# A third buffer for evicted value tiles, inverse roots by Newton's steps on VectorE, and gate and up weights requested ahead of half the tokens

## The chip, the core and the metric

The kernel runs on one core of a Trainium2 chip. TensorE (PE) multiplies matrices into PSUM, VectorE (DVE) and ScalarE (ACT) work on SBUF and PSUM, GpSimd (POOL) works on SBUF, and SyncE (SP) issues most of the transfers. Each engine runs its own instructions in order, and semaphores make it wait for another engine or for a transfer. The metric is the device time of one execution in microseconds; lower is better.

## The reference

Two layers run over 4 sequences of 512 tokens of width 128. Each layer normalizes, runs an attention and a mixture of experts on the same normalized tokens, and adds their gated product:

```
x = L0_attn_x                                   # (4, 512, 128)
xn = _layernorm(x)                              # (x - m) / sqrt(v + 1e-5)
s = _L0_attn_ref(xn, ...)                       # 16 heads, segments of 64, a memory carried on
g = _silu(_L0_ffn_ref(xn, ...))                 # 8 experts, top 2, and a shared one
x = x + s * g
xn = _layernorm(x)
s = _L1_attn_ref(xn, ...)                       # 16 heads, 16 channels of cosine weights
g = _silu(_L1_ffn_ref(xn, ...))                 # 8 experts with gelu, top 2
return x + s * g
```

In the first attention, q, k and v of a sequence are each reshaped to (segments, heads, 64, 64) without a transpose. A segment's output is a sigmoid gate's mix of a softmax attention inside the segment and of a read of a memory M, Z, which elu(k)+1 and v of every segment update.

## The kernel before

**Stages.** Tokens are held as 16 tiles of 128 (`self.x`, tile n belongs to sequence n // 4). First come the layer's first experts (`norm_ffn0`, up to about 76 us of the profile), then the first attention (`attn0`, up to about 300 us) with the second layer's normalization and routing of half the tokens woven in, then the second experts (`ffn1`), then the second attention.

**Loads.** `load_first` (L119) issues, on SP's queue, 12 of the 16 token tiles (the tiles 1, 3, 5, 7 go on ACT's), then `wg` (L136) and `wu` (L138), the gate and up weights of 8 experts, 256 KB each, then `wd` and the attention's weights. `norm_ffn0` needs `wg` at its first expert pair (`glu`, L441) and the tiles 8 to 11 in `sums(2)` after that pair.

**The first attention.** 32 segments n, eight to a sequence, are taken in a loop written out by hand (L834); the order on each engine is the order of the code. A segment's block does: `values(n + 2)` (requests the v of a later segment from DRAM), `scores(n + 1)` (PE `sc`, then DVE `E`, the capped scores), `memory(n)` (PE `mm`, DVE `rm` and `t`, POOL times the gate), `elu` (DVE), `turned` (PE transposes `tn`, which ACT evicts as four `attT` copies and `sk`), `update(n)` (PE `mu`, DVE `mz`), a slot `between.get(n - 0.5)`, `attend(n)` (PE `dot`; DVE `rd`, `t`, `sums`; POOL twice), four chunks of the next projection, a slot `between.get(n - 0.25)`, at n % 4 == 2 `output` (PE `po`, DVE `sg`, POOL adds to `x`), and a slot `between.get(n)`.

**The chunks** are projections for a later group of four segments. At n % 4 == 3 they are four value chunks (`chunk_v`, L616): a matmul `pv` into PSUM, an eviction to an SBUF tile `vt` (by ACT from the third half-sequence on, by DVE before), and a transfer of `vt` to the DRAM tensor `vd`, from where `values` fetches it in another layout. The pool `a0` has two buffers to a tag, so the eviction of the third chunk waits for the first chunk's transfer, and the fourth for the second's. At the other n the chunks are `pp`, of q or k, which ACT evicts to `pj`.

**PSUM.** All of these results share four buffers (`wide`, L347). A matmul group waits until the last reader of its buffer's former content is through, so a late eviction holds up a later matmul that has nothing else to do with it.

**The second norm.** `norm_sums` (L304) takes mean and variance of four tiles in eight DVE instructions. `roots(0, 2)` takes sqrt(v + eps) of eight tiles on ACT, which has to load another function table for it and load the old one again; `scale(0, 2, False)` takes the reciprocal on DVE, and `normed` applies it. The dictionary handed to `attn0` (L2413) says where:

```
18: [(first.sums, 0)], 19: [(first.sums, 1)],
20: [(first.roots, 0, 2)], 20.5: [(first.scale, 0, 2, False), (first.normed, 0)],
21: [(first.turned, 0), (first.normed, 1)],
```

Of the kernel before, what the change touches and what calls it, by code (L numbers as in the profile page):

```python
# [12 lines left out]
F32 = mybir.dt.float32  # L13
I32 = mybir.dt.int32
# [3 lines left out]
ALU = mybir.AluOpType  # L18
# [3 lines left out]
P = 128  # L22
B, S, D = 4, 512, 128
# [3 lines left out]
NT = 16  # L27
EPS = 1e-5
# [80 lines left out]
class Kernel:  # L109
# [8 lines left out]

    def load_first(self, pool, pool_attn, crossed=False):  # L119
        nc, i = self.nc, self.i  # L120
        for n in range(NT):
            eng = nc.scalar if n in (1, 3, 5, 7) else nc.sync
            eng.dma_start(out=self.x[:, n, :], in_=self.tiles_of(i["L0_attn_x"], n))

        self.wr = pool.tile([P, NE], F32, name="wr")
        nc.gpsimd.dma_start(out=self.wr, in_=i["L0_ffn_Wr"])
        self.ebias = pool.tile([P, NE], F32, name="ebias")
        nc.gpsimd.dma_start(out=self.ebias, in_=i["L0_ffn_expert_bias"].partition_broadcast(P))
        self.sg = pool.tile([P, 128], F32, name="sg")
        nc.gpsimd.dma_start(out=self.sg, in_=i["L0_ffn_Sg"])  # L130
        self.su = pool.tile([P, 128], F32, name="su")
        nc.gpsimd.dma_start(out=self.su, in_=i["L0_ffn_Su"])
        self.sd = pool.tile([P, D], F32, name="sd")
        nc.gpsimd.dma_start(out=self.sd, in_=i["L0_ffn_Sd"])
        self.wg = pool.tile([P, NE, F0], F32, name="wg")
        nc.sync.dma_start(out=self.wg, in_=i["L0_ffn_Wg"].rearrange("e d f -> d e f"))  # L136
        self.wu = pool.tile([P, NE, F0], F32, name="wu")
        nc.sync.dma_start(out=self.wu, in_=i["L0_ffn_Wu"].rearrange("e d f -> d e f"))  # L138
        self.wd = pool.tile([P, NE // 2, D], F32, name="wd")
        nc.sync.dma_start(  # L140
            out=self.wd, in_=i["L0_ffn_Wd"].rearrange("(j e) f d -> (e f) j d", e=2)
        )

        self.wqkv = []
        for w in ("Wq", "Wk", "Wv"):
            t = pool_attn.tile([P, H0 * DK], F32, name=f"l0{w}")
            nc.sync.dma_start(out=t, in_=i[f"L0_attn_{w}"])
            self.wqkv.append(t)
        self.wo = pool_attn.tile([P, H0, D], F32, name="l0wo")
        for p in range(2):  # L150
            nc.sync.dma_start(
                out=self.wo[p * 64 : p * 64 + 64],
                in_=i["L0_attn_Wo"].rearrange("(c v) d -> v c d", v=DK),
            )
        be = i["L0_attn_betas"][0, :, 0].rearrange("(hp a p) v -> a p hp v", a=2, p=2)
        self.gate = pool_attn.tile([P, 4, 2, DK], F32, name="gate")
        for p in range(2):
            for a in range(2):


                for x in range(2):
                    rows, cols = (a, slice(x, 4, 2))
                    if crossed:
                        rows, cols = (a + x) % 2, slice(2 * a, 2 * a + 2)
                    nc.sync.dma_start(
                        out=self.gate[rows * 64 : rows * 64 + 64, cols, p, :],
                        in_=be[a, p, x:4:2].partition_broadcast(64),
                    )
# [141 lines left out]

    def norm_root(self, mv, rstd, tiles):
        self.act1(rstd[:, tiles], mv[:, tiles, 1], AF.Sqrt, bias=self.eps)

    def norm_scale(self, mv, rstd, tiles, root=True):
        if root:
            self.norm_root(mv, rstd, tiles)
        self.vec1(self.nc.vector.reciprocal(rstd[:, tiles], rstd[:, tiles]))
# [261 lines left out]
    def attn0(self, xnT, g0, stack, between):  # L579
# [4 lines left out]
        nc, tc = self.nc, self.tc  # L584
# [4 lines left out]
        pool = stack.enter_context(tc.tile_pool(name="a0", bufs=2))  # L589
# [9 lines left out]
        for k in range(4):  # L599
            t = pool.tile([P, 4, 2, DK + 1], F32, name=f"vone{k}", bufs=1)  # L600
# [5 lines left out]
        def project(h):  # L606


            if h >= 2 * B:
                return []  # L610
            qkv[h] = dst = [
                pool.tile([P, 32, 64], F32, name=f"pj{h}_{wi}", tag=f"pj{wi}")
                for wi in range(2)
            ]
            vd[h] = drams.tile([2, P * 16, DK], F32, name=f"vd{h}", tag="vd")
            def chunk_v(p, k):  # L616
                ps = self.narrow(f"pv{h}_{p}_{k}")
                self.mm1(
                    ps, lhsT=xnT[h // 2][:, h % 2 * 2 + p, :],
                    rhs=self.wqkv[2][:, k * S : (k + 1) * S], start=True, stop=True,  # L620
                )
                t = pool.tile([P, S], F32, name=f"vt{h}_{p}_{k}", tag="vt")
                if h > 1:
                    self.act1(t, ps, AF.Copy)
                else:
                    self.vec1(nc.vector.tensor_copy(t, ps))
                nc.sync.dma_start(
                    out=vd[h][p].rearrange("(q k c) d -> k q (c d)", k=2, c=8)[k], in_=t
                )

            def chunk(wi, cq):
                ps = self.narrow(f"pp{h}_{wi}_{cq}").rearrange("p (c k) -> p c k", c=4)
                for c4 in range(4):
                    c = cq * 4 + c4
                    for p in range(2):
                        self.mm1(
                            ps[halves[p], c4, :],
                            lhsT=self.wqkv[wi][:, c * 64 : c * 64 + 64],
                            rhs=xnT[h // 2][:, h % 2 * 2 + p, :], start=True, stop=True,
                        )  # L640
                view = dst[wi].rearrange("d k (t c) -> d (k t) c", c=16)
                self.act1(
                    view[:, :, cq * 4 : cq * 4 + 4], ps.rearrange("d c k -> d k c"), AF.Copy
                )
            qk = [(lambda wi=wi, cq=cq: chunk(wi, cq)) for wi in (1, 0) for cq in range(4)]
            v = [(lambda p=p, k=k: chunk_v(p, k)) for p in range(2) for k in range(2)]
            return v + qk if h else qk[:4] + v + qk[4:]

# [232 lines left out]
    def begin_ffn1(self, pool, psum, layer, rooms=False):  # L881


        nc, v = self.nc, self.nc.vector
        mv = pool.tile([P, NT, 2], F32, name=f"mv{layer}")
        rstd = pool.tile([P, NT], F32, name=f"rstd{layer}")
# [3 lines left out]
        xnT, acc, xn, hid, out = {}, {}, {}, {}, {}  # L890
        parts, picked, place, ids, rows, sent, got, marks = ({} for _ in range(8))
        if rooms:
# [4 lines left out]
                out=ones, in_=ones, pattern=[[1, P]], compare_op=ALU.is_ge, fill=0.0,  # L897
# [37 lines left out]
        def roots(first, end):  # L935
            self.norm_root(mv, rstd, slice(first * 4, end * 4))

        def scale(first, end, root=True):
            self.norm_scale(mv, rstd, slice(first * 4, end * 4), root)

# [188 lines left out]
        def joined(b, part):  # L1129
# [5 lines left out]
                self.vec1(v.tensor_add(acc[b], *got[b]))  # L1135

        return SimpleNamespace(**{f.__name__: f for f in (
            sums, roots, scale, normed, turned, hidden, logits, chosen, up, down,
            split, placed, marked, send, up2, down2, fetch, joined,
        )}, xnT=xnT, acc=acc)  # L1140

# [1239 lines left out]
    def run(self):  # L2381
        nc, tc, ctx = self.nc, self.tc, self.ctx
# [14 lines left out]
        with tc.tile_pool(name="wf1", bufs=1) as wf1, tc.tile_pool(name="f1", bufs=1) as f1:  # L2397
# [11 lines left out]
            first = self.begin_ffn1(f1, None, 1, True)  # L2409
            self.four = True  # L2410
            with tc.tile_pool(name="ap0", bufs=1, space=PSUM) as self.banks:
                left = self.attn0(xnT, g0, stack, {
                    18: [(first.sums, 0)], 19: [(first.sums, 1)],  # L2413
                    20: [(first.roots, 0, 2)], 20.5: [(first.scale, 0, 2, False), (first.normed, 0)],
                    21: [(first.turned, 0), (first.normed, 1)],
                    21.5: [(first.turned, 1), (first.split, 1)],
                    21.75: [(first.hidden, 0), (first.hidden, 1)],
                    23: [(first.logits, 0), (first.logits, 1), (first.chosen, 1)],
                    24: [(first.placed, 1)], 25: [(first.chosen, 0)],
                    30.5: [(first.up, 0, 0)],  # L2420
                })
            self.four = False
            with tc.tile_pool(name="ap", bufs=1, space=PSUM) as psum:
# [33 lines left out]
                f = first  # L2457
# [95 lines left out]
```

## Time and profile before

| | us |
|---|---|
| runs | 707.73, 707.6, 710.62 (median 707.73) |
| profiled execution | 707.65 |
| span of its instructions | 705.7 |
| PE, DVE, ACT, POOL busy | 662.5, 498.5, 488.9, 344.7 |
| mean granted TensorE clock | 0.991 |

The profile shows one execution. Instructions carry the line of the kernel that made them, but the recording helpers make most PE and ACT instructions appear under the helpers' lines L336 and L339, so they are told apart by their tiles. Row times count from the span's start. "Idle before" is the time in which the engine stood still before an instruction, with the event that ended it.

### The profile page before, as it was taken

Reading aid. Unit: us, or ns where it says so; the run is one execution under the profiler, and the core shown is the slowest. Engines: PE = TensorE matmul, PEld = TensorE weight load, DVE = VectorE, ACT = ScalarE, POOL = GpSimd, SP = SyncE. Lnnn points to the kernel's source line nnn. Section 1 sums busy time; section 2 is a strip of 40 time slices with the busy share of each in tenths; the row PEclk is TensorE's granted clock in tenths of the full one; section 3 lists DMA queues with packets and bytes.
Section 4 is the critical chain, followed back from the end, with each engine's and each line's share of the span. In section 5 each row is a group of like instructions: output and inputs, shape, how many; then the busy total and the mean of one; then the engine's idle time right before and its main releaser. Section 6 shows DMA issues by size and latency. Waiting matters only on the chain.

```text
span 705.7 us, 23780 instructions
## 1 busy us (share of the span) xinstructions
PE 662.5 (94%) x10120; PEld 412.4 (58%) x10123; DVE 498.5 (71%) x1072; ACT 488.9 (69%) x809; POOL 344.7 (49%) x383
## 2 busy tenths in 40 slices
PE   7999899999999799789999999999999999999995
PEld 3666667977977768767787783332335243422324
DVE  6866375676677567874459223989897999678884
ACT  4533477786876877742553468989997899899850
POOL 7670046667677384783753333411383835230170
PEclk9999999999999998999999999999999999999999
DMA  7740252232232222100034249967949494947300
GB/s 166 161 136 0 69 144 86 55 108 78 63 95 75 63 61 64 33 3 1 1 109 147 75 150 218 260 167 171 242 153 210 115 249 143 217 136 179 76 17 20
DMA packets 85489, 79.72 MB, mean 113 GB/s; under 512 B 42640, under 2 KB 74160, under 8 KB 82304
## 3 DMA queue, kind: packets, MB, share of 16 engines
q1 hardware_dynamic: 82544, 75.39, 40.4%
q0 software_dynamic: 2256, 2.47, 1.8%
q8 instruction: 82, 1.34, 0.8%
q10 hardware_dynamic: 576, 0.26, 0.1%
q14 instruction: 31, 0.25, 0.1%
HBM read 51.62 MB, written 26.21 MB: 110 GB/s over the span
## 4 chain that ended last, share of the span: by engine, by line
PE 65%; ACT 14%; DVE 12%; DMA 3%; issue 2%; SPq 1%; POOL 0%; DVEq 0%; ACTq 0%; POOLq 0%
PE acc L336 10%; ACT e L339 8%; PE eo L336 7%; PE pp L336 7%; PE po L336 5%; PE ph L336 4%; PE b L336 3%; PE s L336 3%; PE pl L336 3%; DMA vd<-vt 2%; PE pg L336 2%; PE pu L336 2%; PE den L336 2%; PE sc L336 1%; DVE elu L689 1%
## 5 line engine op out<-in xcount | busy, mean ns | idle before, releaser
L339 ACT ACTIVATE e<-s 128x1024 f32<-128x1024 f32 x124 | 121.9, 1055 | 14.0 <-PE s L336 12.9
L336 PE MATMUL acc<-e,strip 128*32 128x512 f32 x1000 | 124.5, 598 | 0.9 <-DVE e L1946 0.9
L339 ACT ACTIVATE e<-e 128x1024 f32<-128x1024 f32 x104 | 107.3, 1094 | 0.0
L743 POOL TENSOR_TENSOR t<-t,gate 128x512 f32<-128x512 f32 x32 | 50.2, 1567 | 54.9 <-DVE t L724 54.9
L336 PEld LDWEIGHTS acc<-e,strip 128*32 128x32 f32 x1000 | 28.4, 109 | 70.0 <-issue 58.3
L781 POOL TENSOR_TENSOR t<-t,gate 128x512 f32<-128x512 f32 x32 | 49.6, 1551 | 34.2 <-DVE sums L780 27.7
L689 DVE SCALAR_TENSOR_TENSOR elu<-elu,up 128x512 f32<-128x512 f32 x60 | 46.3, 771 | 11.6 <-ACT up L339 11.4
L339 ACT ACTIVATE pj<-pp 128x512 f32<-128x512 f32 x64 | 38.0, 608 | 15.4 <-PE pp L336 14.1
L339 ACT ACTIVATE h<-ph 128x1024 f32<-128x1024 f32 x20 | 20.5, 1024 | 39.0 <-PE ph L336 32.3
L336 PE MATMUL s<-q,k 64*128 64x512 bf16 x256 | 40.9, 382 | 3.6 <-ACT e L339 3.3
L782 POOL TENSOR_TENSOR t<-t,t 128x512 f32<-128x512 f32 x32 | 42.7, 1333 | 2.5
L336 PEld LDWEIGHTS <-k 64*128 64x128 bf16 x256 | 8.7, 94 | 59.7 <-issue 58.6
L666 DVE TENSOR_TENSOR E<-sc,cap 128x512 f32<-128x512 f32 x32 | 22.0, 688 | 29.5 <-PE sc L336 29.5
L336 PE MATMUL eo<-w_out,h 128*128 128x128 f32 x320 | 39.7, 278 | 0.0
L336 PEld LDWEIGHTS eo<-w_out,h 128*128 128x128 f32 x320 | 37.6, 192 | 3.4 <-issue 2.2
L339 ACT ACTIVATE elu<-pj 128x512 f32<-128x512 f32 x60 | 38.6, 643 | 0.1
L339 ACT ACTIVATE up<-pj 128x512 f32<-128x512 f32 x60 | 38.4, 640 | 0.0
L1727 POOL TENSOR_TENSOR pr<-pr,pr 128x512 f32<-128x512 f32 x14 | 22.6, 1633 | 29.7 <-DVE pr L1722 29.6
L336 PE MATMUL pp<-xnT,l0Wk 128*64 128x128 f32 x512 | 33.4, 289 | 2.4 <-ACT sk L339 1.6
L339 ACT ACTIVATE attT<-tn 128x128 f32<-128x128 f32 x100 | 19.5, 282 | 21.4 <-PE tn L702 20.5
L1634 DVE TENSOR_TENSOR second<-second,first 128x1024 f32<-128x1024 f32 x16 | 27.0, 1693 | 8.7 <-DMA second<-qf 7.3
L336 PEld LDWEIGHTS pp<-xnT,l0Wk 128*64 128x64 f32 x512 | 30.5, 146 | 4.2 <-ACT sk L339 2.6
(346 smaller groups left out, 1590.3 us busy)
## 6 DMA issues: line engine op xcount, KB each, us to landing
vd<-vt SPq DMA_DIRECT2D x32, 256.0 KB
vone<-vd SPq DMA_DIRECT2D x64, 128.0 KB
first<-qe SPq DMA_DIRECT2D x8, 1024.0 KB
second<-qf SPq DMA_DIRECT2D x16, 512.0 KB
third<-qf SPq DMA_DIRECT2D x32, 256.0 KB
qf<-qT SPq DMA_DIRECT2D x64, 64.0 KB
k<-kd SPq DMA_DIRECT2D x16, 256.0 KB
q<-qd SPq DMA_DIRECT2D x16, 256.0 KB
```

The costliest lines, as they stand in the source:

```text
L336: return self.pin(self.nc.tensor.matmul(*args, **kw))
L339: return self.pin(self.nc.scalar.activation(*args, **kw))
L666: self.vec1(nc.vector.tensor_tensor(e, ps[:, :, 0:256].rearrange("p x (hp c) -> p x hp c", hp=4), bc(bc(self.cap, 1, 4), 1, 2), ALU.min,))
L689: self.vec1(nc.vector.scalar_tensor_tensor(t, t, 1.0, up, ALU.min, ALU.add))
L743: nc.gpsimd.tensor_mul(t, t, self.gate)
L781: nc.gpsimd.tensor_mul(t, t, gate2)
L782: nc.gpsimd.tensor_add(t, t, seg[n]["t1"])
L1634: self.vec1(self.nc.vector.tensor_mul(t, t, self.first1[mm][:, two]))
L1727: self.nc.gpsimd.tensor_add(self.prod1[b, m], self.prod1[b, m], t)
```

## The change

The third edit moves the requests of the tiles 8 to 15 behind those of `wg` and `wu`. The first gives the tag `vt` three buffers in place of two. The second moves `sums(0)` from the end of segment 18 to the end of segment 14, moves `sums(1)` from the end of segment 19 to the slot before its `attend`, drops the square root and the reciprocal, and puts `newton` in the slot before `attend(20)`.

```
@@ load_first
-        for n in range(NT):
-            eng = nc.scalar if n in (1, 3, 5, 7) else nc.sync
-            eng.dma_start(out=self.x[:, n, :], in_=self.tiles_of(i["L0_attn_x"], n))
+        def tokens(first, end):
+            for n in range(first, end):
+                eng = nc.scalar if n in (1, 3, 5, 7) else nc.sync
+                eng.dma_start(out=self.x[:, n, :], in_=self.tiles_of(i["L0_attn_x"], n))
+        tokens(0, 8)
...
         nc.sync.dma_start(out=self.wu, in_=i["L0_ffn_Wu"].rearrange("e d f -> d e f"))
+        tokens(8, NT)
@@
+    def norm_newton(self, pool, mv, rstd, tiles, name):
+        v, n = self.nc.vector, tiles.stop - tiles.start
+        var, r = mv[:, tiles, 1], rstd[:, tiles]
+        half, t = (pool.tile([P, n], F32, name=f"{w}{name}") for w in ("half", "newt"))
+        self.vec1(v.tensor_scalar(half, var, EPS, -0.5, ALU.add, ALU.mult))
+        bits = pool.tile([P, n], I32, name=f"bits{name}")
+        self.vec1(v.tensor_scalar(t, var, EPS, None, ALU.add))
+        self.vec1(v.tensor_scalar(bits, t.bitcast(I32), 1, None, ALU.arith_shift_right))
+        self.vec1(v.tensor_scalar(
+            r.bitcast(I32), bits, -1.0, float(0x5F3759DF), ALU.mult, ALU.add
+        ))
+        for _ in range(3):
+            self.vec1(v.tensor_mul(t, r, r))
+            self.vec1(v.tensor_mul(t, t, half))
+            self.vec1(v.scalar_tensor_tensor(r, t, 1.5, r, ALU.add, ALU.mult))
@@ chunk_v
-                t = pool.tile([P, S], F32, name=f"vt{h}_{p}_{k}", tag="vt")
+                t = pool.tile([P, S], F32, name=f"vt{h}_{p}_{k}", tag="vt", bufs=3)
@@ begin_ffn1
+        def newton(first, end):
+            self.norm_newton(pool, mv, rstd, slice(first * 4, end * 4), f"{first}")
@@ run
-                    18: [(first.sums, 0)], 19: [(first.sums, 1)],
-                    20: [(first.roots, 0, 2)], 20.5: [(first.scale, 0, 2, False), (first.normed, 0)],
+                    14: [(first.sums, 0)], 18.5: [(first.sums, 1)], 19.5: [(first.newton, 0, 2)],
+                    20.5: [(first.normed, 0)],
```

## The prediction

> **What bounds the kernel now.** I read the page first. PE is busy 94% of the span and makes 65% of the chain that ended last, but the chain also holds ACT, DVE and transfers, so the question is where PE waits.
>
> ```profile
> PE 662.5 (94%) x10120; PEld 412.4 (58%) x10123; DVE 498.5 (71%) x1072; ACT 488.9 (69%) x809; POOL 344.7 (49%) x383
> PE 65%; ACT 14%; DVE 12%; DMA 3%; issue 2%; SPq 1%; POOL 0%; DVEq 0%; ACTq 0%; POOLq 0%
> ```
>
> The view of waits, for PE from 112 to 260 us and for ACT from 76 to 300, names what the edits aim at: ACT stands 11.5 us in front of value evictions until a transfer has read the buffer, and PE then stands for ACT (`dot <- ACT vt`, `pp <- ACT sk`).
>
> ```profile
> PE pp L336 <- ACT sk L339: 3.7, 5, 2.1
> PE dot L336 <- ACT vt L339: 3.4, 3, 1.6
> ACT vt L339 <- DMA vd<-vt: 11.5, 9, 2.5
> ```
>
> The timeline shows the worst place, segments 19 to 21 (start, length, engine): two evictions wait 1.12 and 2.49 us, `dot` starts 1.56 late, then ACT is late at every step, and two table loads around one square root make PE wait 2.06 more.
>
> ```profile
> 228.36 0.60 ACT L339 ACTIVATE vt<-pv 128x512 f32<-128x512 f32 x1 [1.12 <-DMA vd<-vt]
> 231.45 0.60 ACT L339 ACTIVATE vt<-pv 128x512 f32<-128x512 f32 x1 [2.49 <-DMA vd<-vt]
> 232.10 1.04 PE L336 MATMUL dot<-vone,E 64*64 64x65 f32 x32 [1.56 <-ACT vt L339]
> 233.07 4.97 PE L336 MATMUL pp<-xnT,l0Wk 128*64 128x128 f32 x64
> 238.71 1.28 ACT L339 ACT_TABLE_LOAD   x1
> 240.31 1.28 ACT L339 ACT_TABLE_LOAD   x1
> 243.95 1.31 PE L336 MATMUL pp<-xnT,l0Wq 128*64 128x128 f32 x20 [2.06 <-ACT sk L339]
> ```
>
> The windows view (PE, PEld, DVE, ACT, POOL busy, granted clock, transfers) says why those 64 `pp` took 4.97 us and not 3.7 as elsewhere: after the pause the clock fell to half.
>
> ```profile
> 233.00:234.00 1.00, 1.00 (x17) 0.93 (x12) 0.88 (x2) 1.00 (x6) 0.00 (x0) 0.50 0.60 223
> 267.00:268.00 1.00, 1.00 (x21) 0.88 (x23) 0.90 (x9) 0.38 (x2) 0.00 (x0) 0.50 0.55 207
> ```
>
> At the start the timeline shows PE waiting for `wg`, requested at 8.91 behind twelve token tiles.
>
> ```profile
> 8.91 0.59 SPq L136 DMA_DIRECT2D wg<-in_L_ffn_Wg_dram  x1
> 13.51 1.12 PE L336 MATMUL pg<-xnT,wg 128*128 128x512 f32 x2 [1.79 <-DMA wg<-in_L_ffn_Wg_dram]
> ```
>
> **The change part by part.** Each place is retimed by hand: rows keep their lengths and start when their last input or their engine is there.
>
> *Weights sooner: -1.15 us.* Tiles take 0.60 us each on SP, so after four of them `wg` is requested at about 3.4 instead of 8.91. It took 4.56 us to land with a full queue; even doubled it lands at 12.5, and at the same speed at 8.0, before PE is free at 11.72. PE then starts `pg` 1.75 us sooner. The second matmul group behind it, `eo`, needs `hs`, which DVE ends at 14.66, so some 0.6 is given back: `pg` of the next pair goes from 17.40 to about 16.25. From there to 63.9 PE is the whole chain, and the gain stays. What moves behind: the tiles 8 to 15, each two requests (1.2 us) later, the last before 10; `sums(2)` reads them at about 17. `wd` and all later requests on SP keep their places, and POOL's and ACT's queues are untouched. Bounds: 0 (another input is late) to -1.75.
>
> *Three tiles.* With three buffers the third eviction waits for nothing and the fourth for the first transfer, where before it waited for the second.
> - First half-sequence (DVE evicts): the third and fourth ran at 84.44 after a wait of 1.37, and PE's transposes at 86.64 waited 0.67 for the `elu` behind them. The fourth alone still starts at 84.44, so `elu` ends 0.7 sooner: -0.65.
> - Segments 3 and 11: ACT's fourth eviction goes from 121.66 to 119.32 (the first transfer lands at 119.28). PE's stalls 0.91 (`dot`) and 0.47 (`pp`) go; PE is the bound again: -1.38 each.
> - Segment 7: PE's stalls are 0.35 (`tn`) and 0.32 (`pp`), and both go: -0.7.
> - Segment 15: see the next item. Segment 23: `vt` waits there too, but PE's `lp` and DVE's routing come last: 0.
> Bounds: 0 (the waits move one tile on) to all the waits of ACT, -11.5.
>
> *`sums(0)` from 18 to 14.* Eight DVE instructions from 221.19 to 222.79 stand between `sg` and `E`. Without them PE's `pv` (224.51) starts 223.72, as `dot` follows `mu` at 223.10: -0.8. The same 1.6 us now stands after `sg` at 194.76: `E` starts 196.36 and not 194.98, `t` ends 197.93, and `pv`, whose PSUM buffer `t` frees, starts 198.08 and not 196.59: +1.5. Behind it the waits for `vt` in segment 15 (0.34 and 0.34 on PE) are gone with the three tiles, so PE is 0.95 late when segment 16's `pp` go on. Net for segment 15: +0.95.
>
> *Segments 19 to 21, with `sums(1)` and the roots moved: -5.5 with the 0.8 above.* `sums(1)` now stands before `attend(19)`: DVE 224.4 to 226.0, so its `t` ends 227.1. Queued behind it are `rd`, `t`, `elu` and `E`; PE's next `sc`, which in the changed program takes the buffer that `t` frees, is due at 227.35: hidden by the `pv`. The first transfer lands 2.06 after its request, at 227.55, so the fourth eviction ends 228.2, and `dot(20)` starts 229.7 and not 232.10. The 64 `pp` take 3.7 at full clock: `sc` at 234.0, not 237.97.
> Newton's 13 instructions follow `mz` at 231.0. The trace has no such instruction; the nearest are 128x8 ones on DVE:
>
> ```profile
> 276.50 0.17 DVE L1052 TENSOR_SCALAR many<-own 128x8 f32<-128x8 f32 x1
> 276.71 0.17 DVE L1054 TENSOR_TENSOR sums<-sums,many 128x8 f32<-128x8 f32 x1
> 276.79 0.16 DVE L1057 SCALAR_TENSOR_TENSOR own<-own,base 128x8 f32<-128x8 f32 x1
> 276.99 0.17 DVE L1058 SCALAR_TENSOR_TENSOR own<-idf,own 128x8 f32<-128x8 f32 x1
> ```
>
> A dependent one starts 0.20 to 0.21 after the one before, an independent one 0.08. Twelve of 13 depend: 12 x 0.21 + 0.08 = 2.6, the value I take. Bounds: 13 x 0.08 = 1.0, and 13 x 0.80 = 10.4 at the pace of `xn` while POOL runs (below). Behind it stands `attend(20)`, whose `t` ends 234.9; `mm(21)` now takes that buffer and is due at 234.55: 0.35 lost. ACT, without two loads and the root (238.69 to 241.60: 2.9 us), ends `sk` at 237.6, and the `pp` that waited 2.06 starts 238.45 and not 243.95. That is -5.5, and the DVE chain `xn`, `E` behind it (249.50) moves as much.
>
> *Sum:* -1.15 - 0.65 - 1.38 - 0.7 - 1.38 + 0.95 - 5.5 = -9.8. After 260 us PE is the chain but for short waits that move with it. 707.65 - 9.8 = 697.85, told as 697.9; the profiled execution stands 0.08 under the median, so this serves for both.
>
> **The rivals.**
>
> *The slow clock also goes at 266 to 273.* The rows there grant 0.70, six times 0.50 and 0.88, 3.4 us lost. It begins after 1.9 us of narrow `lp` matmuls. For: the pause at 230.5 halved the clock, one of 2.06 us at 241.9 did not, so where a pause falls counts, and all of this moves by 9.8 us. Against: two of three runs agree within 0.02%. Time 697.9 - 3.4 = 694.5. The Trainium skill (TensorE: Matmul & The Clock Gate, Part 1: The HAM clock gate) has the clock set by a free-running window of about 3.4 us; the two stretches here, 3.4 and 6.9 us, agree.
>
> *The new pauses cost more.* PE's new 1.5 us at segment 15 halves the clock as at 232 (0.36 + 0.50 + 0.50 + 0.34 = 1.7 us), and Newton takes 0.40 an instruction (the 128x64 row at 275.83 takes 0.38), 5.2 in all, so that `mm(21)` stands 2.6 longer: 697.9 + 4.3 = 702.2.
>
> *The third tile does nothing,* as transfers run one after another and the fourth eviction waits as long as before. For: the second landed 2.3 to 3.1 after the first. Against: the fourth now waits for the first. Lost are 1.38 + 0.7 + 1.38 + 0.5 and, at segment 20, about 2.6: 704.5.
>
> *DVE and POOL block each other: slower.* For: four `xn` take 3.20 us beside POOL's work and 1.11 without it (the timeline at 246.38 and 244.23), 0.52 more each.
>
> ```profile
> 246.38 3.20 DVE L945 TENSOR_SCALAR xn<-x,mv,rstd 128x128 f32<-128x128 f32 x4
> ```
>
> The 16 instructions of the moved sums and Newton's 13 now stand before what feeds POOL. At +0.52 each, 29 x 0.52 = 15.1, all on the chain: 697.9 + 15.1 = 713.0; it decides from 9.8 / 29 = 0.34 an instruction. Against: POOL is idle or waiting for DVE at most of 231 to 235. The Trainium skill (SBUF — State Buffer, Who interferes with whom) speaks against the change here: it states that a VectorE instruction with two SBUF inputs and a GpSimd one that reads SBUF shut each other out for a whole instruction. The row of `xn` agrees in kind.
>
> **How the numbers follow.** Forecast 0.58; clock 0.12; pauses 0.13; third tile 0.10; POOL 0.07. The time is 697.9, its own range 695.5 to 701. Reaching to the clock's case and the pauses' holds 0.83: 694 to 703. This kernel's measurement can tell some 0.5%, 3.5 us, from no change, so faster means under 704.2: 0.58 + 0.12 + 0.13 and half of the third tile's 0.10 make 0.88; the other half and 0.01 of POOL's are no change, 0.06; slower 0.06.
>
> **What would show it.** `pg` at about 11.8; third evictions without a wait and fourth ones some 2.3 us sooner in segments 3 and 11; no half clock at 232; 13 small DVE rows over about 2.6 us before `rd(20)`; no table load between 76 and the `gT` rows; `E` some 1.4 late in segment 15. The forecast is wrong if the stalls on PE return under another name, above all `pv <- DVE t` or `mm <- DVE t` of more than a microsecond.

## The result, and the profile after

The changed kernel takes 697.28 us (median of 4 runs, 696.21 to 700.04) beside 707.66 for the kernel before: a ratio of 0.9866, 95% interval 0.9844 to 0.9888. In two more comparisons, on two chips, the same kernel had 0.9862 (0.9846 to 0.9877) and 0.9837 (0.982 to 0.9854). The execution profiled here is the slowest of its four, 700.04 us with a span of 698.3.

The page, engines and the chain of waits: PE's busy time has hardly changed (662.5 to 661.1), the span is shorter, and PE's share of the chain has gone from 65% to 72%.

```profile
PE 661.1 (95%) x10120; PEld 411.8 (59%) x10123; DVE 501.1 (72%) x1084; ACT 487.1 (70%) x806; POOL 347.7 (50%) x383
...
PE 72%; DVE 15%; ACT 10%; issue 2%; DMA 1%; POOL 0%; SPq 0%; DVEq 0%; ACTq 0%; POOLq 0%
```

The view of waits of the changed kernel, PE from 112 to 260 us and ACT from 76 to 300 (total, times, longest): ACT's 11.5 us for transfers are 2.5, PE waits for no `vt` and no `sk` any more. What is new is a wait of `dot` in segment 24 for `E` (in the kernel before, this `dot` stood at 269.27, outside the window, and waited 0.29 us) and one of `pp` for which the profile names nothing ("issue").

```profile
PE dot L356 <- DVE E L686: 1.9, 1, 1.9
PE pp L356 <- issue: 1.7, 3, 1.3
...
ACT vt L359 <- DMA vd<-vt: 2.5, 5, 0.6
```

The timeline of segments 19 to 21 of the changed kernel (start, length, engine). The fourth eviction waits 0.45 and not 2.49, `dot` does not wait, no table load stands there, both groups of 64 `pp` take 3.71 us, and the pause of 1.28 stands in front of the first.

```profile
222.21 0.60 ACT L359 ACTIVATE vt<-pv 128x512 f32<-128x512 f32 x1 [0.45 <-DMA vd<-vt]
224.17 0.65 PE L356 MATMUL dot<-vone,E 64*64 64x65 f32 x32
226.10 3.71 PE L356 MATMUL pp<-xnT,l0Wk 128*64 128x128 f32 x64 [1.28 <-issue]
232.56 3.71 PE L356 MATMUL pp<-xnT,l0Wq 128*64 128x128 f32 x64
```

The start (SP's queue, then PE): `wg` is requested at 3.73 and not 8.91, and `pg` goes on without a wait.

```profile
3.73 0.60 SPq L138 DMA_DIRECT2D wg<-in_L_ffn_Wg_dram  x1
...
11.62 1.02 PE L356 MATMUL pg<-xnT,wg 128*128 128x512 f32 x2
```

How far PE is ahead of the profile of before at the same instruction, in us, with the steps of the prediction. The second column of measurements is another execution of the changed kernel.

| stage | predicted | this profile | another execution |
|---|---|---|---|
| weights (second `pg`) | 1.15 | 0.95 | 1.81 |
| first half-sequence | 0.65 | 0.72 | 0.69 |
| segment 3 | 1.38 | 1.58 | 1.58 |
| segment 7 | 0.7 | 0.38 | 0.66 |
| segment 11 | 1.38 | 1.86 | 1.86 |
| segments 14 to 17 | -0.95 | -0.10 | 0.18 |
| segments 18 to 21 | 5.5 | 4.49 | 4.39 |
| together at `dot(22)` | 9.8 | 9.76 | 11.36 |

(Steps of at most 0.3 between the stages are left out.) In this profile 1.28 of the 9.87 us that it has at `dot(28)` are lost again by `dot(31)`, where the clock is halved from 297 to 301, and 1.2 more by the end. The other execution has no halved clock before 691 us and took 694.66.

### The profile page after: what moved, and what is told of

The parts are those of the page before. It is cut to its first block, busy times and chain, and to the rows that moved or that the text cites. A ratio compares the mean times of both kernels' runs of the same rounds, so it can differ in the third digit from the quotient of the medians.

```text
span 698.3 us, 23785 instructions
## 1 busy us (share of the span) xinstructions
PE 661.1 (95%) x10120; PEld 411.8 (59%) x10123; DVE 501.1 (72%) x1084; ACT 487.1 (70%) x806; POOL 347.7 (50%) x383
## 3 DMA queue, kind: packets, MB, share of 16 engines
q8 instruction: 82, 1.34, 0.8%
## 4 chain that ended last, share of the span: by engine, by line
PE 72%; DVE 15%; ACT 10%; issue 2%; DMA 1%; POOL 0%; SPq 0%; DVEq 0%; ACTq 0%; POOLq 0%
PE acc L356 10%; ACT e L359 8%; PE eo L356 7%; PE pp L356 7%; PE po L356 6%; PE ph L356 4%; PE pv L356 4%; PE b L356 4%; PE s L356 3%; PE pl L356 3%; PE den L356 2%; PE pg L356 2%; PE dot L356 2%; PE pu L356 2%; PE sc L356 2%; DVE elu L709 2%
## 5 line engine op out<-in xcount | busy, mean ns | idle before, releaser
L763 POOL TENSOR_TENSOR t<-t,gate 128x512 f32<-128x512 f32 x32 | 52.8, 1650 | 54.2 <-DVE t L744 54.2
L801 POOL TENSOR_TENSOR t<-t,gate 128x512 f32<-128x512 f32 x32 | 50.1, 1565 | 24.2 <-DVE sums L800 20.6
L356 PE MATMUL pp<-xnT,l0Wk 128*64 128x128 f32 x512 | 31.5, 280 | 2.6 <-issue 1.7
L356 PE MATMUL po<-l0wo,attT 64*128 64x128 f32 x512 | 31.9, 281 | 0.3 <-DVE t L744 0.3
```

Source lines behind the costliest of these rows:

```text
L356: return self.pin(self.nc.tensor.matmul(*args, **kw))
L763: nc.gpsimd.tensor_mul(t, t, self.gate)
L801: nc.gpsimd.tensor_mul(t, t, gate2)
```

## The experiments

The edits one by one, then parts of them undone, then three tests of what was left. Each ratio is to the kernel before on the same chip.

| kernel | median us | ratio, 95% interval |
|---|---|---|
| weights alone | 704.73 | 0.9965 (0.995 to 0.998) |
| third tile alone | 700.08 | 0.9893 (0.9874 to 0.9912) |
| norm alone | 703.15 | 0.994 (0.9919 to 0.9962) |
| changed kernel, same chip as these | 697.22 | 0.9862 (0.9846 to 0.9877) |
| `sums(0)` back at 18 | 696.36 | 0.9845 (0.9823 to 0.9866) |
| square root kept | 698.4 | 0.9871 (0.9851 to 0.9891) |
| Newton's steps beside POOL | 698.81 | 0.989 (0.9871 to 0.991) |
| `chosen(1)` later | 695.21 | 0.9834 (0.9818 to 0.985) |
| routing sooner | 698.72 | 0.9866 (0.9845 to 0.9887) |
| 16 tiny matmuls more | 701.58 (one run) | none |
| 96 tiny matmuls more | 703.23 (one run) | none |
| changed kernel, same chip as the last three | 696.03 | 0.9837 (0.982 to 0.9854) |

### Weights alone

The third edit on the kernel before.

```
-        for n in range(NT):
...
+        tokens(0, 8)
...
         nc.sync.dma_start(out=self.wu, ...)
+        tokens(8, NT)
```

> Before with the third edit alone (wg and wu requested ahead of the tiles 8 to 15). Theory, as in the prediction: the first pg starts at about 11.8 and not 13.51, the second pair some 1.15 us sooner, and nothing after it changes: 1.0 to 1.2 us less than before, a ratio of about 0.9985. Rival: the lead is used up by the time of the first attention, because another input (wd, or the tiles 8 to 15 themselves, now later) ends the wait: ratio 1.000.

The first `pg` starts at 10.70, the second pair 1.90 sooner than in the profile of before, and the lead is still 1.43 in segments 14 to 20. The time fell by 2.7 us, more than forecast. Two things add to the 0.95. The warm-up matmuls ahead of everything take 5.0 to 6.5 us from execution to execution; without the edit `pg` waits for `wg` either way (13.25 to 13.51), with it a short warm-up is worth the difference (10.70 here, 11.62 in the profile above). And in one of the three profiled executions that wait for `wg`, that of the kernel with the third tile alone, the granted clock is 0.50 from 15 to 18, behind the wait. That the wait halved it is not shown: the two others have no such stretch.

```profile
13.33 1.12 PE L336 MATMUL pg<-xnT,wg 128*128 128x512 f32 x2 [2.35 <-DMA wg<-in_L_ffn_Wg_dram]
```

With the weights alone the clock at 232 to 236 was not halved either, although PE stood there nearly as long in front of `dot(20)`, 1.45 and not 1.56. That made 1.0 us of lead between `dot(19)` and `dot(21)` out of nothing that the edit touches.

```profile
230.56 0.70 PE L339 MATMUL dot<-vone,E 64*64 64x65 f32 x32 [1.45 <-ACT vt L342]
```

### Third tile alone

```
-                t = pool.tile([P, S], F32, name=f"vt{h}_{p}_{k}", tag="vt")
+                t = pool.tile([P, S], F32, name=f"vt{h}_{p}_{k}", tag="vt", bufs=3)
```

> Before with the first edit alone (three tiles of vt). Theory: the waits of ACT for vd<-vt and PE's waits behind them go in the first half-sequence and segments 3, 7, 11 and 15 (0.65 + 1.38 + 0.7 + 1.38 + 0.7 = 4.8 us), and in segment 20 dot's 1.56 us and the half clock behind it (1.7): about 8 us less, ratio 0.989. Rival (the third tile does nothing, transfers follow each other too closely): ACT still waits near 11 us in all, ratio 1.000. Rival (the half clock stays, only places of waits move): 5 us less, ratio 0.993.

7.3 us, and evictions wait 2.6 us and not 12.9 for `vd<-vt` over the kernel (ACT and DVE together): the rival without an effect falls. By place the lead grows by 1.83 in segment 3, 0.35 in 7, 1.86 in 11, 0.87 in 15 and 16, and 2.82 in 18 to 21; there the half clock is gone, as with the weights alone, and the table loads with PE's 2.06 us behind them are still in it.

### Norm alone

```
-                    18: [(first.sums, 0)], 19: [(first.sums, 1)],
-                    20: [(first.roots, 0, 2)], 20.5: [(first.scale, 0, 2, False), (first.normed, 0)],
+                    14: [(first.sums, 0)], 18.5: [(first.sums, 1)], 19.5: [(first.newton, 0, 2)],
+                    20.5: [(first.normed, 0)],
```

> Before with the second edit alone (sums moved, Newton's steps in place of the root, two tiles of vt). Theory: the two table loads and PE's 2.06 us behind them go, DVE has 1.6 us less ahead of E in segment 18, Newton costs 2.6 us of DVE; the vt waits stay, with dot's 1.56 us and the half clock at segment 20: 1.5 to 3 us less, ratio 0.996 to 0.998. Rival: Newton's steps and the sums on DVE take back what the table loads gave, because DVE is the chain from segment 19 to 21: ratio 1.000 or more. If the three edits add up, the three gains together make the 9.8 us that the changed kernel gained by the end of the first attention; if two of them remove the same stall, they make more than that.

4.3 us, above the 1.5 to 3. The lead grows by 3.75 in segments 18 to 21 and not before. With the sums out of the way, the fourth eviction of segment 19 waits 0.42 even with two tiles, `dot(20)` does not wait, and the clock is not halved. So two edits remove the same stall: 2.7 + 7.3 + 4.3 = 14.3 us one by one, 10.2 together on the same chip. In segments 18 to 21 it is 2.82 + 3.75 = 6.6 against 4.4 to 4.5. Each of these leads holds the 1.0 that the weights alone got there from the clock; without it, 4.5 stand against 3.4. So the common stall explains about 1.1 of the 4.1 us that are missing; where the rest went was not followed.

### The changed kernel on the same chip

> The changed kernel again, for the comparison on the same chip: ratio 0.986 to 0.989, with a span of 694 to 698 us that goes up with the time that the clock is halved. If the clock is what spreads the executions, span minus the half-clock time is the same in all of them within 1 us.

The ratio came as expected; the guess on the clock did not. Span times (1 - mean granted clock) taken off the span leaves 690.5 to 692.7 in four executions, 2.2 us apart and not 1: a halved clock is paid in part where PE would have waited anyway. For 266 to 273 the comparison of the rivals below shows it.

### `sums(0)` back in segment 18

```
-                    14: [(first.sums, 0)], 18.5: [(first.sums, 1)], 19.5: ...
+                    18: [(first.sums, 0)], 18.5: [(first.sums, 1)], 19.5: ...
```

> The changed kernel with sums(0) back at the end of segment 18. By the prediction this is 0.95 us better in segment 15 and 0.8 worse in segment 18: 0.1 us less than the changed kernel, nothing that can be measured. By the trace of the changed kernel (pv of segment 15 stood 0.34 us for E and nothing else) moving it cost about 0.3 and should have gained 0.8: 0.5 us more. Either way the row to look at is pv behind E: 1.5 us late, or 0.34.

The time cannot tell the two; the traces can. Against the other execution of the changed kernel this one gains 0.6 from `dot(14)` to `dot(18)` and loses 1.2 from there to `dot(22)`. The changed kernel's rows show why the 1.5 us of the prediction were 0.34 (DVE, then PE): `E` is 1.95 after `sg`, as forecast, but `pv` starts 0.05 after `E` ends. It waits for the buffer that `E` reads, not for the one of `t`, which ends at 192.52.

```profile
189.01 0.42 DVE L828 TENSOR_TENSOR sg<-po,g 128x256 f32<-128x256 f32 x1 [1.23 <-PE po L356]
...
190.96 0.66 DVE L686 TENSOR_TENSOR E<-sc,cap 128x512 f32<-128x512 f32 x1
...
191.67 3.82 PE L356 MATMUL pv<-l0Wv,xnT 128*128 128x512 f32 x8 [0.34 <-DVE E L686]
```

### The square root kept

```
-                    14: [(first.sums, 0)], 18.5: [(first.sums, 1)], 19.5: [(first.newton, 0, 2)],
-                    20.5: [(first.normed, 0)],
+                    14: [(first.sums, 0)], 18.5: [(first.sums, 1)],
+                    20: [(first.roots, 0, 2)],
+                    20.5: [(first.scale, 0, 2, False), (first.normed, 0)],
```

> The changed kernel with the square root on ACT and the reciprocal on DVE (end of segment 20 and before attend(21), as before the change) in place of Newton's steps; the sums stay where the change put them, three tiles stay. Theory: the two table loads stand 2.9 us on ACT at the end of segment 20 and PE waits 2.06 us for sk behind them, and DVE gets 2.6 us back, which takes away the pauses of 1.28 us (pp behind mz) in segment 20: 0.5 to 2 us more than the changed kernel, ratio to before 0.987 to 0.990. Rival (table loads are the main part of the gain of the second edit, DVE's time costs nothing): 2.5 us more or above. Rival (DVE is the chain there and Newton gives all of it back): the same or less than the changed kernel.

PE's wait behind the table loads is back, with the length that it had before:

```profile
235.22 2.84 PE L356 MATMUL pp<-xnT,l0Wq 128*64 128x128 f32 x48 [2.06 <-ACT sk L359]
```

1.5 us of lead go at that place (1.10 behind the other execution of the changed kernel at `dot(21)`, 2.62 at `dot(22)`). The ratio, 0.9871, is the expected one, but its interval overlaps that of the changed kernel, so the time alone shows no loss. Against what was expected, the pause of 1.28 did not go with Newton's steps: it is 1.27 here. So what DVE does behind `mz` is not its cause. `mz` itself is not ruled out by this kernel: it ends 0.10 ahead of `pp` here and 0.12 in the changed kernel.

### Newton's steps beside POOL

```
-                    ... 19.5: [(first.newton, 0, 2)],
+                    ... 19: [(first.newton, 0, 2)],
```

> The changed kernel with Newton's 13 steps one place sooner, at the end of segment 19, where POOL multiplies for 4.7 us without a pause. Rival of the prediction (DVE and POOL block each other, 0.52 us an instruction): the steps take 13 x 0.7 = 9 us and the kernel is 6 us slower than the changed one, ratio to before 0.995. Theory: instructions of 8 elements a row take 0.20 each beside POOL too, except where one has to wait out an instruction of POOL (the first step of the changed kernel took 0.63): the steps take 2.6 to 4.5 us and the time is that of the changed kernel within 2 us.

The steps take 4.6 us (220.81 to 225.41) and not 2.9, far from the rival's 9; its ratio of 0.995 falls with them. Two of the 13 are long, the others 0.16 or 0.17 (timelines of DVE, POOL and PE of this kernel):

```profile
220.81 1.25 DVE L322 TENSOR_SCALAR half<-mv 128x8 f32<-128x8 f32 x1
...
222.16 1.24 DVE L325 TENSOR_SCALAR bits<-newt 128x8 int32<-128x8 int32 x1
...
220.35 1.68 POOL L801 TENSOR_TENSOR t<-t,gate 128x512 f32<-128x512 f32 x1 [2.23 <-DVE sums L800]
222.10 1.27 POOL L802 TENSOR_TENSOR t<-t,t 128x512 f32<-128x512 f32 x1
...
226.06 1.14 PE L356 MATMUL dot<-vone,E 64*64 64x65 f32 x32 [3.16 <-DVE E L686]
```

Both end 0.03 after the instruction of POOL that was under way (222.03 and 223.37). So these instructions of DVE wait out one of POOL; the price is the rest of that instruction, not 0.52 for each. Behind PE's pause of 3.16 the clock is halved from 226 to 229, and the kernel keeps a loss of 2.8 us of lead against the other execution of the changed kernel. The time, 698.81, is too near to the others on that chip to show it.

The same rule read back into the changed kernel (DVE and POOL, segments 20 and 21): `elu` takes 1.25 and 1.57 where every one in segments 18 to 21 of before took 0.68 or 0.69 (the first line is of before), the first `xn` 1.47 and not 1.11, and Newton's first step 0.63. Newton's step ends 0.03 behind POOL's row, each `elu` 0.55 behind it.

```profile
242.78 0.69 DVE L689 SCALAR_TENSOR_TENSOR elu<-elu,up 128x512 f32<-128x512 f32 x1 [2.45 <-ACT up L339]
...
224.13 1.25 DVE L709 SCALAR_TENSOR_TENSOR elu<-elu,up 128x512 f32<-128x512 f32 x1
225.91 0.63 DVE L322 TENSOR_SCALAR half<-mv 128x8 f32<-128x8 f32 x1
...
232.02 1.57 DVE L709 SCALAR_TENSOR_TENSOR elu<-elu,up 128x512 f32<-128x512 f32 x1
...
234.13 1.47 DVE L968 TENSOR_SCALAR xn<-x,mv,rstd 128x128 f32<-128x128 f32 x4
...
223.55 1.28 POOL L802 TENSOR_TENSOR t<-t,t 128x512 f32<-128x512 f32 x1
224.79 1.72 POOL L763 TENSOR_TENSOR t<-t,gate 128x512 f32<-128x512 f32 x1
...
231.77 1.28 POOL L802 TENSOR_TENSOR t<-t,t 128x512 f32<-128x512 f32 x1
```

The Trainium skill (SBUF — State Buffer, Who interferes with whom) says that whoever issues first has the shared ports for the whole instruction; these rows agree. The statistics of `sums` beside POOL keep their 0.26 to 0.29. The trace of before had shown it elsewhere: six of its `elu` take 1.03 to 1.79, the one at 198.40 the longest.

### `chosen(1)` later

```
-                    23: [(first.logits, 0), (first.logits, 1), (first.chosen, 1)],
+                    23: [(first.logits, 0), (first.logits, 1)], 23.5: [(first.chosen, 1)],
```

> The changed kernel with chosen(1), the choice of experts of half the tokens, moved from the end of segment 23 to before attend(24): 2.8 us of small DVE instructions stand behind E, rm, t, elu and mz of segment 24 and no longer ahead of them. Theory: dot(24), which waits 1.94 us for E, goes on at once, and rd(24) is 2.8 us late, which the four chunks behind it hide in part: 1 to 1.9 us less than the changed kernel, ratio to before 0.984. If the half clock follows pauses of PE of about 2 us, it is less often seen at 259 to 268. Rival (DVE is the chain there, the wait moves to the next matmul behind t): no change.

`dot(24)` goes on at once, 2.1 us sooner, and PE then waits 0.85 and 2.04 at the next two places where DVE is late:

```profile
262.15 0.69 PE L356 MATMUL sc<-pj,pj 64*64 64x64 f32 x32 [0.85 <-DVE t L744]
...
266.62 0.70 PE L356 MATMUL dot<-vone,E 64*64 64x65 f32 x32 [2.04 <-DVE E L686]
```

By `sc(28)` all of the 2.1 is gone, part of it under a halved clock from 268 to 271. So the wait moved on, as the rival has it. The median is the lowest of all kernels, but it was not run beside the changed kernel on one chip, and the ratios overlap: no gain is shown.

### The pause in front of `pp`: more instructions ahead

`t` ends 0.6 us ahead of where `pp` could have started. `mz` ends 0.10 to 0.15 ahead of `pp` in seven of the eight executions with this pause; only with norm alone `pp` goes on 0.66 before `mz` starts. The page has a queue of instructions (packets, MB, share):

```profile
q8 instruction: 82, 1.34, 0.8%
```

1.34 MB in 82 packets is 16 KB each; PE's 20,243 recorded instructions make that 66 bytes an instruction at most, some 250 to a packet. In all eight executions PE goes on 1.34 to 1.46 us after the end of such a packet (2.3 to 2.9 after its start). Two kernels add tiny matmuls behind the warm-up, which changes nothing in the code of segment 20 but should shift the packets' borders in it.

```
+            for _ in range(16):
+                self.mm1(pw[0:32, 0:4], lhsT=warm[:, 0:32], rhs=warm[:, 0:4], start=True, stop=True)
```

> The changed kernel with 16 tiny matmuls (4 columns) behind the warm-up: 32 more PE instructions (a matmul and a weight load each) ahead of all else. What is asked is the pause of 1.28 us ahead of pp in segment 20, for which the profile names no releaser (t, elu and mz of DVE end at other distances from it in other kernels, a packet of the instruction queue always 2.4 to 3.0 us before it). Theory: PE waits for its own instructions, which come in packets of 16 KB = 256 instructions, and outruns one packet where sc, mm, tn, mu and dot stand close together (288 instructions in 2.9 us); then the pause stays 0.8 to 1.5 us long but falls 32 instructions sooner, inside dot(20) and no longer ahead of pp. Rival (a wait for DVE, POOL or a buffer that the profile doesn't name): the pause stays ahead of pp with 1.28 us.

The pause is as long, 1.26, and stands exactly 32 instructions sooner (16 matmuls with their weight loads), inside `dot(20)`:

```profile
227.05 0.41 PE L356 MATMUL dot<-vone,E 64*64 64x65 f32 x16
228.72 0.46 PE L356 MATMUL dot<-vone,E 64*64 64x65 f32 x16 [1.26 <-issue]
```

The second has 96 in place of 16.

> The same with 96 tiny matmuls, 192 more PE instructions; their own time stands at the start of the kernel (3 to 10 us) and is not the question. Theory: the packet's border falls in mm of segment 20, and the packet before it holds dot(19) and the slow pv (3.7 us for 16 instructions), so PE doesn't outrun it: no pause over 0.4 us ahead of pp or inside segment 20; segment 20 takes about 1.2 us less from sc(21) to sc(22) than the 7.82 us of the changed kernel. Rival (a wait for DVE, POOL or a buffer): the pause is there with 1.28 us.

The pause is gone, and `sc(21)` to `sc(22)` takes 6.48 us, not 7.83. `pp` starts at 229.60, and `mz` ends at 230.83, so `mz` is out as a cause. But a wait for DVE takes the place of the pause at once:

```profile
229.02 0.65 PE L356 MATMUL dot<-vone,E 64*64 64x65 f32 x32
229.60 3.71 PE L356 MATMUL pp<-xnT,l0Wk 128*64 128x128 f32 x64
...
234.80 0.70 PE L356 MATMUL mm<-mz,elu 64*64 64x65 f32 x32 [0.86 <-DVE t L746]
```

From `sc(21)` to `sc(23)` both take the same, 15.36 and 15.38. So the pause is PE waiting for its own instructions, and it costs nothing here, because DVE sets the time behind it.

It is not the only one. Inside `dot(28)` the kernel before and all the others but these two have a pause of 0.79 to 1.15 us of the same kind, which ends 1.29 to 1.51 us after the end of a packet; with more instructions ahead it is not there. And such a pause need not be free: with 96 matmuls a pause of 0.52 without a releaser stands inside `dot(14)`, where DVE is not late, and PE stays 0.74 further behind from there on.

The two kernels took 701.58 and 703.23 us, one execution each, beside 696.03 for the changed kernel on the same chip. Their second `pg` is 1.8 and 2.8 later than there. In the first one the transfers of `vt` were late in segments 3 and 7: the fourth eviction waited 2.22 and 2.61 in spite of three tiles, and PE 0.91 and 1.58 behind it. So the third tile's gain hangs on the transfers' speed; why they were late in this execution is not known.

### Routing sooner

```
-                    23: [(first.logits, 0), (first.logits, 1), (first.chosen, 1)],
-                    24: [(first.placed, 1)], 25: [(first.chosen, 0)],
+                    22: [(first.logits, 0), (first.logits, 1)], 22.5: [(first.chosen, 1)],
+                    23.5: [(first.chosen, 0)], 24: [(first.placed, 1)],
```

> The changed kernel with the routing of the second layer one segment sooner: logits at the end of segment 22, chosen(1) before attend(23), chosen(0) before attend(24), placed(1) as before at the end of 24. DVE is idle for some 6 us from 245 to 260 and is what PE waits for from 258 to 275 (1.94, 0.82, 0.30 and 0.99 us). Theory: these waits go, less what segments 22 and 23 lose to the lp matmuls and the choice standing ahead of pv: 2 to 3 us less than the changed kernel, ratio to before 0.981 to 0.983. Rival (DVE is the chain from 258 to 295, the place within it doesn't matter, as the kernel with chosen(1) alone moved gave all of its 2.1 us back two segments later): the same as the changed kernel, 0.985 to 0.987.

> The changed kernel a third time, on the same chip as the version above: ratio 0.985 to 0.988.

698.72 beside 696.03 for the changed kernel on the same chip: no gain, and the theory falls; the rival's range, 0.985 to 0.987, holds the ratio. All of its runs are above all of the changed kernel's, but the intervals of the ratios touch. The changed kernel itself came out at 0.9837, a little under the 0.985 to 0.988 that was expected. PE's lead is 1.34 behind the other execution of the changed kernel at `dot(22)`, 0.88 of it from the start of the kernel, and 3.47 behind at `dot(27)`; the waits stand at other places (0.91 at `mm`, 1.99 at `sc`, 1.36 at `dot`), and the clock is halved from 266 to 273 and from 290 to 294. Neither of the two orders gains what PE waits for behind 258 us; no version beats the changed kernel beyond its interval.

## Why the prediction was right, and where it was not

The forecast was 697.9, the measured median 697.28. The lead of 9.8 us that the sum gives is 9.76 at `dot(22)`, behind its last term, in the profile and 11.36 in another execution. That the first of these agrees so well is in part luck: two terms missed by a microsecond each, in opposite directions, and 1.0 of the lead is a half clock of the profile of before that the edits need not have removed.

**Weights, 1.15:** right in kind. 0.93 to 0.95 where the warm-up was long (6.5 us) and 1.79 to 1.90 where it was short (5.0 to 5.6), against a bound of 1.75. The profile of before could not show that the warm-up's length varies.

**Third tile, 0.65 + 1.38 + 0.7 + 1.38:** right; 0.7, 1.58, 0.38 to 0.66, 1.86. The retiming took the waits of PE as they stood in the trace; segments 3 and 11 gave 0.2 and 0.5 more than these waits, and why was not followed.

**`sums(0)` in segment 14, +0.95 net:** the step "`pv`, whose PSUM buffer `t` frees" failed. The buffer is freed by `E`, and the 1.5 us were 0.34. In the old trace `pv` waits for `t` at 224.51, in segment 19; segment 15 is the last of its sequence and has no `mu` between `mm` and `pv`, so the four buffers need not stand alike there. Which reader frees a buffer has to be read for each place from the program.

**Segments 18 to 21, -5.5:** the stalls that it names went, all of them, and the half clock at 232 went too. But the step took that half clock (4.97 us and not 3.7) for a part of what the edits remove, and with the weights alone it went with the stall of 1.45 still there; 1.0 of the 4.4 to 4.5 is that. A pause at this place is then not enough to halve the clock. Beside that, the step is mis-sized by 1.0: it let DVE's chain move with PE at its old lengths. In the changed kernel DVE has no pause from 222.68 to 244, and it is the bound there, as the kernel without the pause shows. Up to `t(20)` the working was right (234.9 forecast; 229.87 + 5.27 = 235.14). Behind it `elu` took 0.89 and the first `xn` 0.36 more, beside POOL: 1.25. Newton's own steps came as told, 0.20 from one to the next, 2.92 in all with the 0.46 that the first waited. The wait of 0.35 at `mm(21)` lay under the pause, and is 0.86 where the pause is gone.

**The rivals.** The third tile does nothing: fell (ratio 0.9893 alone), though in the one execution with 16 matmuls more the waits were there again in two segments. DVE and POOL block each other: the mechanism is there, at about 0.57 + 0.46 + 0.89 + 0.36 = 2.3 us and not 15.1, since the moved small instructions, all but Newton's first, found POOL idle or were of a kind that POOL doesn't block; three of the four rows that paid were large ones that the change only shifted. The new pauses cost more: the 1.5 at segment 15 never came, nor did the half clock there. The clock at 266 to 273: the stretch is gone, but the price was wrong. None of three profiled executions of the changed kernel has that stretch of 3.4 us lost; two have pieces of 1.7 us lost elsewhere, at 259 and 297 in the first and at 294 in the third. In the second and third of these executions and with `sums(0)` back at 18, where no piece falls near it, PE's lead grows by 0.66 from `dot(23)` to `dot(25)`, and not by 3.4, since PE then waits 1.93, 0.82 and 0.30 there for DVE.

**The signs named beforehand.** `pg` at 11.62, fourth evictions 4.0 and 5.9 us sooner in segments 3 and 11, of which 1.66 and 3.51 is lead that they had already and 2.35 the third tile's, `E` 1.3 late in segment 15 (190.96 against 194.98 - 5.33), no table load between the one at 80.16, which stood at 81.10 before, and the pair around the `gT` rows: all there. The warning sign, a stall of over a microsecond under another name, came too, as `pp <- issue`; it turned out to cost nothing there, because DVE sets the time behind it.

## What to carry to other kernels

Edits that remove waits at one place don't add up: in segments 18 to 21 two of them cleared the same stall. And what one old trace shows of the clock is one execution's: take it out of the price of a stall unless a second execution has it too. After retiming one engine, ask which engine is then without a pause, and check its long rows against the neighbour that will now run beside it: rows keep their lengths only while their company stays the same. And test a pause without a releaser by moving it; if it goes where the instruction count goes, it isn't a wait for data.

## What the runs showed of the hardware

**PE can wait for its own instructions.** They come in 16 KB packets, and where 288 instructions follow each other in 2.9 us behind a slow stretch of 16 in 3.7 us, PE stood 1.05 to 1.43 us and went on 1.3 to 1.5 us after the end of a packet. Adding 32 instructions moved the pause by 32, adding 192 removed it. When a packet is asked for was not measured.

**Some instructions of DVE that meet one of POOL under way end with it or after it**: 128x8 TENSOR_SCALAR steps of 0.17 took 1.25 and 1.24 and ended 0.03 behind POOL's, and `elu`, which reads two tiles in SBUF, took 1.03 to 1.79 and not 0.68. Statistics (0.26 to 0.29), reciprocals (0.20) and instructions with an input in PSUM (all 28 `mz`, 0.68 to 0.69) were not held up.

**The halved clock comes in pieces of 1.7 us lost.** Twelve of fourteen profiled executions have one or more before their last 10 us, as (1 - granted clock) summed over the windows: 1.68 to 1.71 or twice that. One such window of the profile above, from the view by windows (PE, PEld, DVE, ACT, POOL busy, granted clock, transfers):

```profile
260.00:261.00 1.00, 1.00 (x32) 0.90 (x32) 0.90 (x3) 0.00 (x0) 0.12 (x1) 0.50 0.07 16
```

The place changes between the three executions of the changed kernel (259 and 297; 294; none). The Trainium skill (TensorE: Matmul & The Clock Gate, Part 1: The HAM clock gate) has a free-running window of about 3.4 us; 3.4 us at half speed is 1.7, so the runs agree. A pause of 1.9 us at the same instruction was followed by it in one execution (259) and not in two others, and in front of `dot(20)` a pause of 1.56 was followed by it and one of 1.45 was not.
